# Which queue carries the turned output columns: two layers of a graph network on one core

## The chip, the core and the metric

The kernel runs on one core of a Trainium2 chip. A core has five engines that matter here, each with an instruction stream of its own that it works through in order: TensorE (PE, matmuls), VectorE (DVE), ScalarE (ACT), GpSimd (POOL) and SyncE (SP), which only issues transfers. Transfers (DMA) between the chip's main memory and the core's on-chip memory are carried by 16 DMA engines. A transfer is issued by an instruction in the stream of SP or of ACT, so it takes a place in that engine's order and can wait there. Transfers issued by SP are on queue q1 of the profile, those of ACT on q10. An engine waits for others through semaphores.

The metric is the device time of one execution in microseconds (us); the median of several runs counts.

## The reference

The input is x, 3327 rows of 512 numbers, and adj, a 3327 x 3327 matrix. Everything is in 32-bit floats. Two layers follow each other:

```python
# layer 0
h = relu(layernorm(x))
q, k, v = h @ Wq.T + bq, h @ Wk.T + bk, h @ Wv.T + bv
a = q @ k.T / sqrt(512) + adj + adj
x = x + softmax(a) @ v                      # called x1 below
# layer 1
h = relu(layernorm(x))
A2 = adj + I;  d = diagonal(A2) ** -0.5
temp = A2 @ h @ W.T
x = x + relu((d[:, None] * A2 * d[None, :]) @ temp)
```

So there are three large products with a 3327 x 3327 matrix: the softmax's with v (the kernel applies Wv after it), A2 with h, and A2 with temp. The change concerns the end of the last one, where x1 is added and the output is written.

## The kernel before, in words

The 3327 rows are padded to 26 tiles of 128. They are divided into two strips (of 14 and 12 tiles), and each strip into two halves (`HT` = 7 and 6 tiles, so 896 and 768 columns). `ROW` maps the kernel's tile order to rows.

**The three products.** Each large product (`g` = 0, 1, 2) is computed by a scheme with seven block products instead of eight, applied twice, one inside the other. The outer seven are named in `ORDER` (p5, p1, p6, p7, p2, p3, p4). For each of them and each strip `s` the kernel makes seven steps: `t` = 0 to 5, which take a pair of tiles each, and `t` = None for the thirteenth tile. That is 3 x 7 x 2 x 7 = 294 steps, numbered k = 0 to 293 by `number_of(g, r, s, t)`. A step with a pair issues the seven inner products at line 918, one with the thirteenth tile four products at line 909. Each product shows as two matmul records per weight tile, so x14 or x8 per step. A step's operand tiles (`a`) are read from main memory by `left`: line 829, 832 or 836, two transfers of 384 or 448 KB a step on SP. They land in a ring of five slots. VectorE makes sums of them (`four_sums`, lines 163 to 165) in a ring of three slots. The other factor (`Right.load` and `Right.rows`, lines 856 and 870; `Right.make`) is loaded on SP during the second strip of the product before and the first steps of the first strip, and reused in the second strip.

**Gathering.** At the end of a strip (steps t = 5 and t = None) the banks of the accumulator are combined into the result `cts` by VectorE, beginning with a copy by ScalarE (line 961, `Gather.first`; then lines 962 to 965, `Gather.rest` at 981). Some banks are seeded ahead of the next products from `cts` by ScalarE (line 955, `Gather.seed`). The last bank, p8, is seeded only after that copy, as it takes the bank of p1; the product for p8 is the last of the thirteenth tile's four.

**The output columns.** `cts` holds the result turned: features in the partitions, rows of x along the free dimension. During the last two and a half outer products of g = 2 (from step 252 on) most parts of it are final, and class `Columns` writes them out one at a time: 14 parts (s, y, d), one every three steps, the last one two steps behind its predecessor. One part has four methods, entered in the table `between` with the step at which each is due:

- `load` (two steps ahead): the part of x1 is loaded from main memory into one of two slots (`xp_slots`), in the blocked order in which a turn by 32 x 32 blocks leaves the data. Four transfers of 112 or 96 KB, in pieces of 32 numbers, 128 bytes.
- `turn` (the step itself): VectorE transposes the part in 32 x 32 blocks into a slot of `turn_ring`.
- `scale` (one step later): VectorE applies relu and the scale d.
- `add` (two steps later): VectorE adds x1, and four stores to the output, again in pieces of 128 bytes, are handed to `post`.

The six row tiles from 20 on, of which one half of the features is final only at the very end, go another way: `last_load` (line 1104, the x1 rows on ACT), `turn_last` (transposes on TensorE, line 1110) and `finish` (line 1123 on ACT, line 1124 on VectorE, line 1125 a store on SP or ACT in turn).

**The order of work.** `run(k)` writes step k out for all engines. In it come first the operand loads of step k + 3, then all methods of `between` whose name contains "load", then the step's products, then `deliver(k)`, then the gathering and seeding, then the sums of step k + 2 and the other methods of `between`. Everything is inside `in_order`, which holds each engine, SP and ACT among them, to exactly the order in which its instructions were written.

`post` does not issue a transfer but puts it in the list `posted` with the number of the current step. `deliver(before)` takes entries from the head of the list while their number is below `before`. A store posted in step k is so issued in `deliver(k + 1)`, behind the products of step k + 1, on ScalarE (line 795). In ScalarE's order this is ahead of the copy and the seed of step k + 1, if it has any. At the end, `finish` is called for the six tiles and `deliver(len(steps) + 1)` takes what is left.

The slots: `turn_ring` has the slots mid 10 and mid 11, the first two of `spare`. The slot half 11 holds the bias of v in g = 0 and weights of layer 1 in g = 1 (`other_weights`), and nothing afterwards.

Of the kernel before, what the change touches and what calls it, by code (L numbers as in the profile page):

```python
# [47 lines left out]
def graph_layers_kernel(  # L48
# [30 lines left out]
    nc = tc.nc  # L79
# [21 lines left out]
    def ring(*slots):  # L101

        turn = itertools.cycle(slots)

        def take(shape, name):
            kind, k = next(turn)
            return kind(k, shape, name)

        return take
# [213 lines left out]
    class Turned:  # L323
# [23 lines left out]
        def load(self):  # L347
            k, w = self.k, self.w
            self.other = half(2, [P, 2, BW], "a21")[:, :, :w]
            a11, a12, a22 = hp[k][:, 0], hp[k][:, 1], hp[k][:, 2]  # L350
            for y, blocks in enumerate(((a11, a12), (self.other, a22))):
                c0 = ROW[y * HALF + PACKS[k][0]] * P
                xs = xT[:, c0 : c0 + w].rearrange("(z c p) e -> z p c e", z=2, p=P)
                for z, to in enumerate(blocks):
                    after(nc.sync.dma_start(to, xs[z]), self.row)
            self.norms = []
            for m in range(2):
                self.norms.append(half(m, [P, 2, BW], "norms")[:, :, :w])
                self.loaded = nc.sync.dma_start(
                    self.norms[m], normd[k][m][0:1, : 2 * w].rearrange("a (y e) -> a y e", y=2).to_broadcast([P, 2, w]))  # L360
# [415 lines left out]
    def view(k, j):  # L776
        if k not in parts:
            n = PACKS[k][1]
            parts[k] = large(k, [P, n, 4, Q[0]], f"part{k}")
        return parts[k][:, j]  # L780
# [10 lines left out]
    now = [0]  # L791
    posted = []

    def post(dst, src):
        posted.append((now[0], lambda: nc.scalar.dma_start(dst, src)))  # L795
# [13 lines left out]
    spare = [(mid, k) for k in range(10, 15)]  # L809
# [4 lines left out]
    ts_slots = [lambda k=k: view(2, 1).rearrange("p a w -> p (a w)")[:, k * D : (k + 1) * D] for k in range(3)]  # L814
    ts_slots = itertools.cycle([*ts_slots, *(lambda k=k: mid(k, [P, D], "ts") for k in range(12, 15))])
    xp_slots = itertools.cycle([lambda k=k: view(2, 1)[:, 2 * k : 2 * k + 2].rearrange("p a w -> p (a w)") for k in range(2)])
    turn_ring = ring(*spare[:2])
    xr_last = ring(*((half, k) for k in (4, 5, 6)))
    out_last = ring((half, 12), (half, 13), *spare[2:], (half, 14))

# [306 lines left out]
    class Columns:  # L1127
# [10 lines left out]
        def load(self):  # L1138
            self.x = next(xp_slots)()[:, : H[self.s]]
            for to, rows in self.parts(self.x, x1d[self.s][self.y]):  # L1140
                nc.scalar.dma_start(to, rows)

        def turn(self):
            self.o = turn_ring([P, H[0]], "turned")[:, : H[self.s]]
# [8 lines left out]
        def add(self):  # L1153
            nc.vector.tensor_add(self.o, self.o, self.x)
            r0 = (STRIPS[self.s] + self.y * HT[self.s]) * P
            for of, rows in self.parts(self.o, out[r0 : r0 + H[self.s]]):
                post(rows, of)

    every = (*range(PAIRS), None)
    rights = {(g, r, t): Right(g, r, t) for g in range(3) for r in ORDER for t in every}  # L1160
# [555 lines left out]
```

## Time and profile before

| | us |
|---|---|
| median of 3 runs | 2185.3 (2182.72 to 2186.67) |
| the profiled execution's own time | 2186.69 |
| its span in the profile | 2184.8 |
| busy in the span: TensorE matmuls | 2145.7 (98%) |
| VectorE | 1653.1 (76%) |
| ScalarE | 273.0 (12%) |
| GpSimd | 69.1 (3%) |

Transfers: q1 (issued by SP) 276472 packets with 515.02 MB, q10 (issued by ACT) 123936 packets with 69.62 MB. The loads of x1 columns are 56 transfers on q10 between 1922.0 and 2152.0 us, with a median issue time of 538 ns and a median of 5.1 us to land; the stores of columns are 56 transfers on q10 between 1972.3 and 2174.3 us, with a median issue time of 556 ns and a median of 4.5 us to land.

How to read the profile: times are us from the start of the span, unless ns is written. "L918" is line 918 of the kernel. A line of the timeline gives start, duration, engine, line, operation, output<-input with their shape, how many instructions are merged, and in brackets how long the engine was idle before and what ended that. PE is the matmul part of TensorE, PEld its weight load, which overlaps; ACTq and SPq are the instruction queues of ScalarE and SyncE, where transfers are issued. A releaser is inferred from semaphore events, and a wait for several is put down to the one that came last. The tile called `part` in the profile is one region of on-chip memory that serves the operand ring, the sums, the slots of x1 and parts of `cts`; `p` are accumulator banks. "Clock" is the share of the full TensorE clock that was granted, and the DMA share is the mean busy share of the 16 DMA engines; as packets overlap, it can pass 1.

### The profile page before, as it was taken

How to read it: one execution, taken by the hardware profiler on the slowest of the kernel's cores; microseconds unless marked ns; L12 is line 12 of the kernel's file. 1: busy time of each engine (PE TensorE's matmuls, PEld its weight loads, DVE VectorE, ACT ScalarE, POOL GpSimd, SP SyncE). 2: the span in 40 equal slices, each digit the busy share in tenths (PEclk: the TensorE clock that was granted, in tenths of full speed). 3: DMA queues.
4: the chain of work that ended last, by engine and by line, in shares of the span. 5: the costliest groups of instructions: out<-in, count | busy, mean ns of one | idle time of the engine just before them, and what ended most of it. 6: DMA issues, size and time to landing. Idle time of an engine off the chain costs nothing.

```text
span 2184.8 us, 20926 instructions
## 1 busy us (share of the span) xinstructions
PE 2145.7 (98%) x6272; PEld 1183.8 (54%) x6272; DVE 1653.1 (76%) x3235; ACT 273.0 (12%) x441; POOL 69.1 (3%) x63
## 2 busy tenths in 40 slices
PE   9999999999999999999999999999999999999978
PEld 5555555555555555555455555555666655554534
DVE  7479888889977788877777788785656577776876
ACT  6312111212100000001101000001111100000000
POOL 3000000000004000000111000000000000000000
PEclk9999999999999999999999999999999999999989
DMA  8678988889999999889787899886546468789886
GB/s 301 207 254 300 313 298 287 302 294 314 327 261 329 323 357 322 274 292 315 265 315 256 284 328 355 312 280 204 187 142 205 141 205 291 244 224 234 212 225 153
DMA packets 400530, 586.07 MB, mean 268 GB/s; under 512 B 139788, under 2 KB 273304, under 8 KB 400408
## 3 DMA queue, kind: packets, MB, share of 16 engines
q1 hardware_dynamic: 276472, 515.02, 70.7%
q10 hardware_dynamic: 123936, 69.62, 10.9%
q8 instruction: 52, 0.85, 0.2%
q14 instruction: 70, 0.57, 0.1%
HBM read 416.68 MB, written 167.84 MB: 268 GB/s over the span
## 4 chain that ended last, share of the span: by engine, by line
PE 90%; DMA 4%; DVE 3%; ACTq 1%; issue 1%; ACT 0%; SPq 0%; POOL 0%; DVEq 0%
PE p L918 52%; PE Y L541 13%; PE Z L541 7%; PE p L909 4%; PE p L1025 4%; PE pw L1086 3%; PE X L541 3%; PE Y L397 2%; PE Z L397 1%; DMA part<-sum 1%; DMA part<-x1d 1%; DMA part<-in_adjT_dram 1%; ACTq L795 1%; DMA rows<-row 0%; PE X L397 0%
## 5 line engine op out<-in xcount | busy, mean ns | idle before, releaser
L918 PE MATMUL p<-part,b 128*128 128x448 f32 (+1 forms) x3528 | 1263.7, 514 | 7.5 <-ACT p L955 7.0
L918 PEld LDWEIGHTS p<-part,b 128*128 128x128 f32 x3528 | 672.1, 191 | 553.8 <-issue 296.8
L541 PE MATMUL Y<-qt,hp 128*128 128x448 f32 (+1 forms) x832 | 307.9, 513 | 1.9 <-DVE g L553 1.9
L163 DVE TENSOR_TENSOR part<-part 128x896 f32<-128x896 f32 (+1 forms) x252 | 256.8, 1019 | 67.4 <-DMA part<-sum 22.8
L541 PEld LDWEIGHTS Y<-qt,hp 128*128 128x128 f32 x832 | 158.0, 190 | 134.7 <-issue 72.7
L541 PE MATMUL Z<-qt,hp 128*128 128x384 f32 (+1 forms) x416 | 162.2, 512 | 0.0
L165 DVE TENSOR_TENSOR part<-part,part 128x448 f32<-128x448 f32 (+1 forms) x219 | 129.5, 591 | 14.9
L909 PE MATMUL p<-part,b 128*128 128x448 f32 (+1 forms) x336 | 126.2, 518 | 14.4 <-ACT p L955 14.4
L164 DVE TENSOR_TENSOR part<-part,part 128x448 f32<-128x448 f32 (+1 forms) x219 | 129.4, 591 | 7.2
L541 PEld LDWEIGHTS Z<-qt,hp 128*128 128x128 f32 x416 | 79.0, 190 | 66.2 <-issue 37.9
L545 DVE SCALAR_TENSOR_TENSOR g<-g,Y 128x384 f32<-128x384 f32 (+1 forms) x156 | 91.5, 587 | 29.8 <-PE Y L541 26.5
L909 PEld LDWEIGHTS p<-part,b 128*128 128x128 f32 x336 | 64.1, 191 | 69.2 <-issue 31.7
L961 ACT COPY part<-p 128x384 f32<-128x384 f32 (+1 forms) x33 | 16.6, 502 | 678.9 <-PE p L918 384.1
L962 DVE TENSOR_TENSOR part<-p,part 128x384 f32<-128x384 f32 (+1 forms) x33 | 19.3, 586 | 98.4 <-PE p L918 63.4
L548 ACT ACTIVATE g<-g 128x768 f32<-128x768 f32 (+1 forms) x48 | 43.0, 896 | 345.4 <-DVE g L545 301.5
L541 PE MATMUL X<-qt,hp 128*128 128x384 f32 (+1 forms) x208 | 81.1, 512 | 0.0
L1025 PE MATMUL p<-w,ct 128*128 128x512 f32 x136 | 61.6, 592 | 0.0
L541 PEld LDWEIGHTS X<-qt,hp 128*128 128x128 f32 x208 | 39.5, 190 | 33.1 <-issue 19.3
L190 POOL TENSOR_TENSOR rstd<-ve,mhalf 128x1 f32<-128x1 f32 x46 | 39.3, 857 | 529.9 <-DVE ve L188 502.8
L981 DVE TENSOR_TENSOR ct<-p,part 128x448 f32<-128x448 f32 (+1 forms) x72 | 42.4, 610 | 17.5 <-PE p L909 13.2
L1086 PE MATMUL pw<-w,rows 128*128 128x256 f32 x208 | 53.5, 380 | 0.4 <-DVE rows L1076 0.4
L1016 DVE TENSOR_TENSOR job<-job 128x896 f32<-128x896 f32 (+1 forms) x52 | 53.0, 1019 | 0.0
(194 smaller groups left out, 1682.5 us busy)
## 6 DMA issues: line engine op xcount, KB each, us to landing
part<-sum SPq DMA_DIRECT2D x104, 448.0 KB, 5.3
part<-p SPq DMA_DIRECT2D x91, 448.0 KB, 5.7
part<-sum SPq DMA_DIRECT2D x104, 384.0 KB, 3.8
part<-p SPq DMA_DIRECT2D x91, 384.0 KB, 4.7
part<-in_adjT_dram SPq DMA_DIRECT2D x78, 448.0 KB, 5.2
b<-row SPq DMA_DIRECT2D x234, 128.0 KB, 4.9
part<-in_adjT_dram SPq DMA_DIRECT2D x78, 384.0 KB, 3.6
g<-in_adjT_dram SPq DMA_DIRECT2D x52, 448.0 KB, 4.3
```

Of the source, the lines that this page charges most:

```text
L163: yield nc.vector.tensor_add(o[:, 0:2], g[:, 0:4:3], g[:, 1:2].to_broadcast([P, 2, g.shape[-1]]))
L164: yield nc.vector.tensor_add(o[:, 2], o[:, 1], g[:, 0])
L165: yield nc.vector.tensor_add(o[:, 3], o[:, 2], g[:, 2])
L397: nc.tensor.matmul(ps[:, :w], M[B[name]][:, c, o * P : (o + 1) * P], hp[k][:, A[name], c], start=start and c == 0, stop=c == 1, skip_group ...
L541: nc.tensor.matmul(ps[:, :wd], h_of(self.t, name, k), qt[B[name]][:, k], start=start and k == 0, stop=k == 1, skip_group_check=True)
L545: nc.vector.scalar_tensor_tensor(a[n], a[n], 2.0, ps[:, :wd], op0=ALU.mult, op1=ALU.add if sign > 0 else ALU.subtract)
L548: nc.scalar.activation(g[1], g[1], AF.Exp, **({"bias": pad} if self.t == HALF - 1 else {}))
L909: yield nc.tensor.matmul(ps[("p2", "p3", "p4", "p8")[k]][:, :w], b[:, z], a[:, 0, y], start=k == 3 and not self.seeded, stop=True, skip_gr ...
L918: yield nc.tensor.matmul(ps[r][:, :w], b[:, i], m, start=self.t == 0 and not adds, stop=self.t == PAIRS - 1 and r in ("p1", "p5", "p6", "p ...
L1016: nc.vector.tensor_add(self.a, self.a, self.b)
L1025: nc.tensor.matmul(ps, cts[s][y][d][:, k * P : (k + 1) * P], w[d], start=d == 0, stop=d == DC - 1)
L1086: nc.tensor.matmul(ps, a, W[B[name]][:, c], start=new and c == 0, stop=c == 1, skip_group_check=True)
```

## The change

Three edits:

- `turn_ring` gets a third slot, half 11.
- `Columns.load` issues its four loads of x1 on SP instead of ACT. Their place in the written order stays: step k - 2, behind the operand loads of that step and the loads for the right factor.
- `Columns.add` no longer calls `post`, but puts its four stores into `posted` itself, with the number of the current step plus 2, and to be issued on SP. `deliver` takes them three steps after the add instead of one; those of the last column are taken by the call behind the last step. As the list is taken from its head, what is posted behind such an entry waits for it.

```diff
-    turn_ring = ring(*spare[:2])
+    turn_ring = ring(*spare[:2], (half, 11))
@@ class Columns, load
             for to, rows in self.parts(self.x, x1d[self.s][self.y]):
-                nc.scalar.dma_start(to, rows)
+                nc.sync.dma_start(to, rows)
@@ class Columns, add
             for of, rows in self.parts(self.o, out[r0 : r0 + H[self.s]]):
-                post(rows, of)
+                posted.append((now[0] + 2, lambda rows=rows, of=of: nc.sync.dma_start(rows, of)))
```

## The prediction

> **What bounds the kernel now.** I read the busy shares first, then the chain that ended last, then the last third engine by engine.
>
> ```profile
> PE 2145.7 (98%) x6272; PEld 1183.8 (54%) x6272; DVE 1653.1 (76%) x3235; ACT 273.0 (12%) x441; POOL 69.1 (3%) x63
> ```
>
> TensorE works for 98% of the span, so only what keeps it idle or slow can pay. The chain has the matmuls of lines 909 and 918 in a fixed rhythm (start, duration, what):
>
> ```profile
> 1887.52 31.57 PE p L918 x84
> ...
> 1951.77 31.57 PE p L918 x84
> ...
> 2024.32 33.14 PE p L918 x84
> ...
> 2140.48 3.01 PE p L909 x8
> ```
>
> Undisturbed, one product of two strips lasts 1951.77 - 1887.52 = 64.25 us, and its first strip 31.57 + 3.01. From 1951.77 the first strip of the last product should end at 1951.77 + 2 x 64.25 + 34.58 = 2114.85; it ends at 2143.49. **28.6 us are lost**, all where turned columns are loaded and stored. The timeline of PE names the engine:
>
> ```profile
> 2022.67 1.65 PE L909 MATMUL p<-part,b 128*128 128x384 f32 x2 [7.01 <-ACT p L955]
> ...
> 2097.35 1.65 PE L909 MATMUL p<-part,b 128*128 128x384 f32 x2 [7.40 <-ACT p L955]
> ...
> 2109.19 31.28 PE L918 MATMUL p<-part,b 128*128 128x448 f32 x78 [6.18 <-ACT p L955]
> ```
>
> With a wait of 0.20 at 2062.59 that is 20.8 us of waiting; the other 7.8 are slow matmuls behind each wait (two take 1.65 us, where six of the same form took 2.10 before it; x84 take 33.14 instead of 31.57). What ScalarE did meanwhile is in its timeline, where ACTq is its queue of instructions:
>
> ```profile
> 1997.65 5.98 ACTq L795 DMA_DIRECT2D out_dram<-turned  x4
> 2004.84 9.54 ACTq L1141 DMA_DIRECT2D part<-x1d  x4
> 2016.30 5.28 ACTq L795 DMA_DIRECT2D out_dram<-turned  x4
> 2021.62 0.48 ACT L961 COPY part<-p 128x384 f32<-128x384 f32 x1 [32.54 <-DMA out_dram<-turned]
> 2022.13 0.49 ACT L955 ACTIVATE p<-ct 128x384 f32<-128x384 f32 x1
> ```
>
> TensorE finished the step at 2013.57; the copy and the seed for the last bank, half a microsecond each, stood behind eight DMA issues until 2021.62. The four stores were ready from 2003.6 (their add starts at 2002.65): they stood behind the loads, and the loads behind landings, since the chain runs from one landing to the next issue (store issued 1999.18, 5.63 us; loads 2004.84, 7.01 us, and 2011.87, 5.84 us). The transfers are crowded there (length, PE, PEld, DVE, ACT and POOL busy, clock, DMA share, GB/s):
>
> ```profile
> 1750.00:1920.00 170.00, 170.00 (x483) 91.61 (x483) 124.27 (x239) 7.16 (x14) 0.00 (x0) 1.00 0.72 239
> 1983.00:2025.00 42.00, 34.96 (x103) 19.66 (x102) 24.52 (x40) 2.29 (x5) 0.00 (x0) 0.95 1.06 242
> ```
>
> [...] between 1983 and 2016 the column loads take a median 6.8 to 7.0 us to land, over the whole run at best 2.5. [...] I count no byte as saved. [...] columns go in pieces of 128 B. Between 1983 and 2016 q10 moved 1.73 MB with 37.0% of the engines' time and q1 6.77 MB with 72.6%: 4.7 against 9.3 MB per full share, half the rate. [...]
>
> **The change part by part.**
>
> *Loads and stores leave ACT.* 14 columns x 4 = 56 loads and 56 stores. ACT then holds only copies, seeds and, at the end, xr loads and three output stores. The three waits on ACT go, and with them the slow matmuls: -28.6 us. The seed then follows a step's end by copy and seed, 0.49 + 0.49 us, and is needed only after six matmuls of the thirteenth tile, 2.10 us: hidden.
>
> *They join SP.* Median issue 0.54 (load) and 0.56 us (store): 112 x 0.55 = 62 us on SP. Between 1920 and 2180 SP waits 71.8 + 38.0 + 6.8 + 6.1 + 3.0 = 125.7 us for TensorE to free operand slots; that hides the 62 on average. Not everywhere: in 1983 to 2016 these waits are only 12.2 us for some 16 issues (9 us), so the cover is nearly used up. What stands behind them on SP are operand loads (L832, L836) and right factors (L856, L870), for which DVE's sums and then TensorE wait. Their reserve: a load issued at 1998.93 lands for the sum at 2005.93, DVE ends its sums at 2008.4, and TensorE would need them, undelayed, at 2013.57 + 3.01 = 2016.6: **8.2 us**. A column issued at its best, 4 x 0.55 = 2.2 us, is hidden in it; uncovered it would cost 2.2 for each half column.
>
> *DMA time.* Unchanged in bytes, but now in a shorter time. The highest share that holds for some time is 1.12 (1996 to 2016). The stretch 1983 to 2025 carries 1.06 x 42 = 44.5, or 39.7 us at 1.12; TensorE's own work in it is 34.96: 4.8 us too much. 2057 to 2110 carries 0.87 x 23 + 0.93 x 30 = 47.9, or 42.8 us; TensorE's 22.8 + 16.4 less some 3.8 for the slow clock is 35.4: 7.4 too much. Both lie under the reserve of 8.2, so the least is 0; with no reserve it is 12.2 us and about 5 for a slow clock again. I take **+4**, as the second comes close and carries over from the first.
>
> *Stores two steps later.* A store queued in step j is issued in step j+3 of SP's order, whose operand load waits for TensorE to be done with step j+1. DVE's add of step j is over by then, as DVE has to make the sums of step j+2 ahead of it; only after a gather (a step with t = 5) it may be 1 us late. Issued in j+1, the store would hold SP for most of a step (4.5 us): that is the cost if this cover were gone. At nothing.
>
> *Third slot (half 11).* A column is turned every 3 steps; its store is issued 5 steps after its turn and takes a median 3.6 to 5.0 us. Two slots come round after 6 steps, about when it lands; three after 9, some 3 steps (13.5 us) in hand. The slot's earlier tile belongs to the weights of the stage before. Nothing.
>
> *x slots.* Two remain: a load waits for the add of the column before last. Normally that is two steps old; only for the last column one step, where SP may wait up to 4 us, with two operand steps left to load. Nothing.
>
> *Tail.* Now the last four column stores start at 2172.73 on ACT, and the first of six output activations waits for them:
>
> ```profile
> 2172.73 2.42 ACTq L795 DMA_DIRECT2D out_dram<-turned  x4
> 2176.00 1.57 ACT L1123 ACTIVATE r<-pt,sd 128x256 f32<-128x256 f32 x4 [8.78 <-DMA out_dram<-turned]
> ```
>
> Its transposes run from 2173.22 to 2175.38, so ACT can start near 2173.7 and end with them, about 2.4 us earlier; SP's three output stores come behind four column stores (2.2 us), which takes some back: -1.8. Bounds -2.5 and +2.
>
> Sum against the profiled execution, 2186.69 us (span 2184.8): 2186.69 - 28.6 + 4 - 1.8 = 2160.3. That execution is 1.4 above the median of 2185.3; the forecast is **2160**.
>
> **The rivals.**
> - *Transfers take the waits' place* (part of the gain): [...] the reserve doesn't carry. For: shares of 1.06 and over, SP's waits of 12.2 us. Against: DVE's 8.2 us. With the 12.2 + 5 above it gives 2186.7 - 28.6 + 17 - 1.8 = 2173.
> - *SP blocks as ACT did* (slower): the four loads hold SP as long as they held ACT at worst (9.54) and the stores 5.98, 15.5 us a column, beside a dozen other issues of 0.42 (5 us): 20.5 in three steps of 4.52 (13.6), 7 late; with six issues 18 in 15.8, 2 late. Some 7 columns of each kind: 49 + 14 = 63, less 2 x 8.2 reserve, gives 2186.7 - 30.4 + 47 = 2203. It decides once a column holds SP longer than 13.6 - 5 = 8.6 us (15.8 - 2.5 = 13.3 in the loose strips). Against: the pair's medians make 4.4; the long ones on ACT were waits for landings.
> - *No change*: ACT was only the messenger, and the crowded transfers hold seed and operands all the same, so as many microseconds come back on DVE's sums. For: the chain before the first wait is made of landings. Against: the copy was ready to run at 2013.57 whatever landed. 2185.
>
> **How the numbers follow.** Forecast case 0.62 (2152 to 2167: from no late transfer at all, 2156, less the spread of the three runs, to 10 us late); partial 0.21 (2167 to 2181); no change 0.04; slower 0.13. The range 2152 to 2180 leaves out the last two and the edge of the second. A change of 0.2%, 4.4 us, is what this kernel's measurement can tell from none. Faster 0.83, same 0.04, slower 0.13.
>
> **What would show it.** Right: no wait of PE on ACT p L955 above 1 us from 1950 on, PE's rhythm near 64.25 throughout, the last turned stores on SP and the first output activation right behind its transposes. The +4 is right if DVE's L163 or b waits a few us on DMA near the last product's start. Wrong: SP's queue with column issues of 2 us and more each, DVE's sums waiting on part<-in_adjT_dram or b<-row in every third step, and PE waiting for DVE; or new SP waits on DVE's add L1154, which would mean that two steps are too few.

## The result and the profile after

The changed kernel takes 2169.03 us (median of 4 runs, 2168.21 to 2169.72) beside 2184.2 us of the kernel before in the same session: a ratio of 0.9929 with a 95% interval of 0.9912 to 0.9946, so 15 us or 0.7% faster. The profiled execution took 2169.72 us, its span is 2167.9.

The page's first part, and from the chain that ended last the starts of the last five outer products (start, duration, what):

```profile
PE 2142.5 (99%) x6272; PEld 1182.1 (55%) x6272; DVE 1653.3 (76%) x3235; ACT 273.1 (13%) x441; POOL 68.4 (3%) x63
```

```profile
1824.88 31.57 PE p L918 x84
...
1889.13 31.57 PE p L918 x84
...
1953.38 31.57 PE p L918 x84
...
2017.62 31.57 PE p L918 x84
...
2081.87 20.31 PE p L918 x54
```

From 1824.88 to 2081.87 the distance is four times 64.25 us to the hundredth: up to the start of the last product nothing is lost any more. Before, two products in this stretch came 8.3 and 10.4 us late. The timeline of PE shows what is left, all in the last product:

```profile
2109.69 4.78 PE L918 MATMUL p<-part,b 128*128 128x448 f32 x12 [0.76 <-DVE part L164]
2114.31 3.17 PE L909 MATMUL p<-part,b 128*128 128x448 f32 x8
2121.46 30.08 PE L918 MATMUL p<-part,b 128*128 128x384 f32 x84 [3.98 <-DVE part L962]
2151.38 2.74 PE L909 MATMUL p<-part,b 128*128 128x384 f32 x8
```

No wait on ACT p L955 stands there. The two that do are waits for VectorE, and the 84 matmuls behind the second take 30.08 us where they took 27.25 in undisturbed strips.

One measure serves for all runs below. From a product's undisturbed start (1824.88 here) five products of 64.25 us lead to the last matmul of line 909, 321.25 us later. What a run needs beyond that is its **loss**; from there to the end of the span is its **tail**. After: 2151.38 + 2.74 - 1824.88 - 321.25 = 8.0 us lost, and a tail of 2167.9 - 2154.12 = 13.8. Before, from 1823.27: 28.6 lost, and a tail of 11.7. The start itself lies between 1820.5 and 1825.4 in the profiles below, though the kernels do the same work up to there; why single executions differ by that much was not looked into. So a difference in time between two runs is only partly loss and tail.

### The profile page after: what moved, and what is told of

The parts are those of the page before. It is cut to its first block, busy times and chain, and to the rows that moved or that the text cites. A ratio compares the mean times of both kernels' runs of the same rounds, so it can differ in the third digit from the quotient of the medians.

```text
span 2167.9 us, 20907 instructions
## 1 busy us (share of the span) xinstructions
PE 2142.5 (99%) x6272; PEld 1182.1 (55%) x6272; DVE 1653.3 (76%) x3235; ACT 273.1 (13%) x441; POOL 68.4 (3%) x63
## 2 busy tenths in 40 slices
DMA packets 400530, 586.07 MB, mean 270 GB/s; under 512 B 139788, under 2 KB 273304, under 8 KB 400408
## 4 chain that ended last, share of the span: by engine, by line
PE 90%; DVE 5%; DMA 3%; issue 1%; SPq 0%; POOL 0%; ACT 0%; DVEq 0%
PE p L918 52%; PE Y L541 13%; PE Z L541 6%; PE p L909 5%; PE p L1025 4%; PE pw L1086 3%; PE X L541 3%; PE Y L397 2%; PE Z L397 1%; DMA part<-in_adjT_dram 1%; DVE part L163 1%; DMA part<-p 1%; DMA rows<-row 0%; PE X L397 0%; DMA wk<-in_wk_dram 0%
## 5 line engine op out<-in xcount | busy, mean ns | idle before, releaser
L165 DVE TENSOR_TENSOR part<-part,part 128x448 f32<-128x448 f32 (+1 forms) x219 | 129.5, 591 | 14.9
L981 DVE TENSOR_TENSOR ct<-p,part 128x448 f32<-128x448 f32 (+1 forms) x72 | 42.5, 609 | 18.2 <-PE p L909 13.8
```

The costliest lines, as they stand in the source:

```text
L165: yield nc.vector.tensor_add(o[:, 3], o[:, 2], g[:, 2])
```

## The experiments

All kernels of a group ran on one chip with the kernel before beside them. The ratio is to that; loss and tail come from one profile each.

| run | median us | ratio (95% interval) | loss | tail |
|---|---|---|---|---|
| before | 2184 to 2186 | 1 | 28.6 | 11.7 |
| after | 2169.0 | 0.9929 (0.9912 to 0.9946) | 8.0 | 13.8 |
| only the stores moved | 2166.1 | 0.9909 (0.9893 to 0.9926) | 8.4 | 12.9 |
| only the loads moved | 2176.5 | 0.9963 (0.9948 to 0.9977) | 14.9 | 15.1 |
| later stores and third slot, all on ACT | 2181.8 | 0.9974 (0.9964 to 0.9985) | 21.7 | 12.0 |
| after, stores not later | 2181.4 | 0.9977 (0.9966 to 0.9988) | 19.9 | 11.9 |
| after, two slots | 2165.3 | 0.9906 (0.9888 to 0.9923) | 7.8 | 11.3 |
| after, xr loads on SP too | 2164.7 | 0.9900 (0.9883 to 0.9916) | 4.3 | 13.8 |
| before, a quarter of each column transfer | 2159.8 | 0.9875 (0.9856 to 0.9894) | 2.6 | 10.6 |
| after, a quarter of each column transfer | 2158.1 | 0.9868 (0.9852 to 0.9885) | 0.0 | 10.2 |
| after, long pieces | 2162.5 | 0.9887 (0.9870 to 0.9903) | 6.3 | 9.5 |
| xr on SP, last stores not later | 2164.3 | 0.9903 (0.9886 to 0.9919) | 3.8 | 14.2 |
| xr on SP, column loads on GpSimd | 2161.9 | 0.9885 (0.9869 to 0.9902) | 3.9 | 13.5 |
| the last two together | 2161.3 | 0.9880 (0.9863 to 0.9896) | 3.8 | 11.2 |

After reading the changed kernel's trace I had a theory for the remaining loss and a rival. It rests on a listing of the transfers that SP issues near 2104 us in the compiled program (number, line, transfer, semaphores waited for):

```
1560 L1141 DMACopy part2_3621<-x1d10_147 32x24x32 [waits DMAHW1_49,DVE_49]
1561 L1141 DMACopy part2_3621<-x1d10_147 32x24x32 [waits DMAHW3_49]
1562 L1141 DMACopy part2_3621<-x1d10_147 32x24x32 [waits DMAHW1_49]
1563 L1141 DMACopy part2_3621<-x1d10_147 32x24x32 [waits DMAHW2_49]
1564 L836 DMACopy part0_3572<-in_adjT_dram 128x768 [waits DMAHW3_49,PE_49]
```

DMAHW0 to DMAHW7 are eight completion semaphores that this program deals in turn to the transfers of *both* queues. The trace has them as numbers 100, 102 and 104 to 109: all of SP's 1608 transfers and ACT's 194 carry one of these eight, each number occurs on both engines, and 1671 of the 1802 wait, before their issue, on the number that they carry themselves. The five above carry 102, 105, 102, 104 and 105. The numbers skipped (DMAHW2, and 4 to 0; in the trace 104, 106 to 109 and 100) went to the six xr loads, which are still on ACT. So instruction 1562 waits for the landing of 1560: the last update of 102 comes at 2110.22 us and the issue at 2110.24. And 1563 waits for an xr load on another engine: 104 at 2111.81, the issue at 2111.82. The kernel before deals the same eight numbers to SP's 1496 transfers and ACT's 306, and that is how ScalarE came to wait for landings there: its load at 2011.87 waits on 109, which the load issued at 2004.84 updates for the last time at 2011.85. In the trace this is what happened; SP's timeline first, then ACT's, then SP's waits from 2103 to 2113 us (sum, times, longest):

```profile
2103.95 8.18 SPq L1141 DMA_DIRECT2D part<-x1d  x4
2112.23 0.94 SPq L836 DMA_DIRECT2D part<-in_adjT_dram  x2
```

```profile
2108.97 0.53 ACT L961 COPY part<-p 128x448 f32<-128x448 f32 x1 [25.09 <-PE p L918]
2109.53 0.55 ACT L955 ACTIVATE p<-ct 128x448 f32<-128x448 f32 x1
2109.67 2.79 ACTq L1104 DMA_DIRECT2D xr<-x1d  x6
```

```profile
SPq L1141 <- DMA part<-x1d: 5.3, 1, 5.3
SPq L1141 <- DMA xr<-x1d: 1.3, 1, 1.3
```

The xr loads stand behind the step's copy and seed, which wait for TensorE. SP's four column loads took 8.18 us. Of these, 5.3 went by until load 1560 landed, whose semaphore came round so soon because the xr loads had used six; only 1.3 went by waiting for an xr load itself. The operand load behind them went out from 2112.23 on and took 5.7 us to land; VectorE sat idle for it, and that is the 3.98 us of TensorE:

```profile
2118.66 0.96 DVE L163 TENSOR_TENSOR part<-part 128x768 f32<-128x768 f32 x1 [6.09 <-DMA part<-in_adjT_dram]
```

The *ring theory* says that the rest of the loss is this holding of one queue by the other. The *traffic theory* says that SP and the DMA engines are full with small pieces, so that operands are late in any case. The trace has both at once: the wait of 5.3 us comes from the dealing and from a slow landing.

**Which half of the move counts.** The first two runs do one half each.

```diff
# only the stores moved: after, with
-                nc.sync.dma_start(to, rows)
+                nc.scalar.dma_start(to, rows)
```

> Stores on SP, two steps later, with the third slot; the loads of x1 stay on ACT. Ring theory (ScalarE's copy and seed are late because an issue ahead of them waits for the landing of an earlier transfer of either queue): the loads alone still hold ACT, but end earlier, since no store stands between them and the copy; one or two waits of PE on the seed of 1 to 4 us remain, 2174 us. Traffic theory [...]: SP has half of the added issues, so operands are on time and the last product has no wait of PE on DVE, 2165 us.

```diff
# only the loads moved: before, with
-                nc.scalar.dma_start(to, rows)
+                nc.sync.dma_start(to, rows)
```

> Loads of x1 on SP, stores as before on ACT one step after the add, two slots. Ring theory: the stores are ready when ACT comes to them, but wait for landings and hold the copy by one group (5 us) where the add comes just before it; one or two waits of PE on the seed, 2174 us, and the tail of before (first output activation behind the last store). Traffic theory: 2165 us, no wait of PE on DVE in the last product.

Stores alone on SP are as good as both: 2166.1 us, loss 8.4. The time is next to the traffic theory's 2165, though its "no wait on VectorE" fails: there is one of 2.4 us. The waits on the seed that the ring theory wanted are there too, but small (two on ACT p L955, 3.4 us in all), and its 2174 is missed. Loads alone leave more than half as much to lose as before (14.9 of 28.6): the ring theory's 2174 is nearer to 2176.5 than the rival's 2165, and the waits on the seed are 1.17 and 4.45 us. So either half takes issues away from in front of the copy. The stores look like the better half, but the first run also has the later stores and the third slot, and the second has neither; the next run shows that these two alone are worth 4 to 6 us, which is part of the 10 us between the halves.

**The later stores.** First alone on ACT, then the changed kernel without them.

```diff
# later stores and third slot on ACT: before, with
-    turn_ring = ring(*spare[:2])
+    turn_ring = ring(*spare[:2], (half, 11))
-                post(rows, of)
+                posted.append((now[0] + 2, lambda rows=rows, of=of: nc.scalar.dma_start(rows, of)))
```

> The kernel before with only the later stores and the third slot; loads and stores stay on ACT. If ACT's lateness came from waiting for the add of a column: gone, below 2170 us. Traffic theory (it comes from landings that are slow because the small pieces fill the engines, and as many issues stand before the copy): PE's waits on the seed stay above 10 us in all, 2180 to 2186 us.

```diff
# stores not later: after, with
-                posted.append((now[0] + 2, lambda rows=rows, of=of: nc.sync.dma_start(rows, of)))
+                posted.append((now[0], lambda rows=rows, of=of: nc.sync.dma_start(rows, of)))
```

> The changed kernel with the stores posted with the current step's number, so issued on SP one step after the add instead of three. SP runs ahead of VectorE, so each group of stores makes it wait for the add, at most most of a step (4.5 us), 14 times; with operands late in the crowded stretches: ring theory 2190 us, with SP waiting on L1154 for 30 us and more in all. Traffic theory: the same transfers in nearly the same time, 2170 us.

On ACT the delay and the third slot bring 4 us by the medians and 6 by the ratio, and TensorE still waits 7.21, 9.17 and 0.51 us for the seed, 16.9 of 20.8: ACT's lateness was for the most part not the wait for an add. On SP the delay is worth 10 us by the ratios and 12 by the medians; the runs without it lie far apart (2174.9 to 2188.9). SP's list of waits without it:

```profile
SPq L1157 <- DVE turned L1154: 31.4, 7, 11.3
```

That is the 30 us expected, 24.0 of it up to 2140 us; the changed kernel has 6.2 us of it in two waits, both at the very end, when no operand load is left. The loss grows by 11.9 us (19.9 against 8.0), so a good part of the waits falls into slack. The delay isn't all that differs in the profile: SP also waits 8.2 us for xr loads before column loads, where it waits 1.3 in the changed kernel.

**The third slot.**

```diff
-    turn_ring = ring(*spare[:2], (half, 11))
+    turn_ring = ring(*spare[:2])
```

> The changed kernel with two slots for turned tiles again. A slot then comes round after six steps and its store is issued five steps after the turn, so the turn of column n waits for the landing of the stores of column n-2: VectorE waits for it up to a landing (5 us) where SP is late, and its sums with it. Traffic theory: SP is late in the last two products, so this bites, 2180 us. If the slots were never short: 2169 us.

The loss is the same, 7.8 against 8.0. VectorE waits for a landing of stores twice, for 1.26 and 0.97 us, inside its slack. The profiled execution is shorter by an earlier start (1821.43) and a shorter tail, and the intervals of the two ratios overlap: the third slot gains nothing that these runs show.

**What holds the last product.** The xr loads go to SP; then the pieces are made fewer, or longer. Where a transfer brings only a quarter, the slots are cleared once at the start.

```diff
# xr loads on SP too: after, with
-            nc.scalar.dma_start(xr[:, k], x1_of(i + k)[:, 0:E])
+            nc.sync.dma_start(xr[:, k], x1_of(i + k)[:, 0:E])
```

> The changed kernel, with the six xr loads (line 1104) on SP too, so that ScalarE issues no transfer before the last outputs. Ring theory (SP stood from 2104.9 to 2112.2 because its transfers waited for semaphores that the xr loads held, and these waited in ACT for a step's end): the waits of PE on DVE of 0.76 and 3.98 us and the slow matmuls behind them go, 2169.0 - 7.5 = 2161.5 us. Traffic theory (SP and the DMA engines are full there in any case): 2167 to 2170 us, the waits of PE stay.

The 3.98 us wait becomes three of 0.2 to 0.5, and the loss falls from 8.0 to 4.3; by time alone the gain is not clear, as the intervals of the two ratios touch. It is half of what the ring theory promised. TensorE still waits 0.67 us for a seed and 1.20 for VectorE, and VectorE is idle for an operand load for 2.34 us at 2116.20 instead of 6.09. SP's timeline has the column loads and the first xr loads:

```profile
2104.63 6.11 SPq L1141 DMA_DIRECT2D part<-x1d  x4
2135.77 0.90 SPq L1104 DMA_DIRECT2D xr<-x1d  x2
```

The four column loads still hold SP for 6.11 us, where they held it for 8.18, and SP's list of waits has none over 2.2 us for an xr load. And the edit does more than free the semaphores. ACT had run ahead and issued the xr loads at 2109.67; in SP's order they come 26 us later, so their 0.79 MB are also gone from the stretch where the late operand load lands. These runs don't tell the two apart.

```diff
# a quarter of each column transfer, on before and on after
+    primed = []
...
-        return [(tile[32 * a : 32 * a + 32].rearrange("r (j e) -> r j e", e=32), rows[self.d, a]) for a in range(4)]
+        q = HT[self.s]
+        return [(tile[32 * a : 32 * a + 32].rearrange("r (j e) -> r j e", e=32)[:, 0:q], rows[self.d, a, :, 0:q]) for a in range(4)]
...
             self.x = next(xp_slots)()[:, : H[self.s]]
+            if len(primed) < 2:
+                primed.append(nc.gpsimd.memset(self.x, 0.0))
```

> The changed kernel with every column transfer cut to a quarter: as many transfers, each with a quarter of its 128-byte pieces (three quarters of x1 aren't added and three quarters of these output columns aren't stored). Traffic theory (the rest of the loss in the changed kernel is the small packets' time on the DMA engines): the last product's waits go and the time is 2157. Ring theory alone (the rest is SP standing behind the xr loads of ScalarE): SP still stands until the step's end near 2109, a wait of PE of some 2 us and slow matmuls remain, 2161 to 2163.

> The kernel before with every column transfer cut to a quarter, as in the run above (three quarters of x1 aren't added and three quarters of these columns aren't stored); the order and the number of transfers on ACT and SP stay. If ACT is late because the landings it waits for are slowed by traffic: the waits of PE on the seed shrink from 20.8 us to under 5, 2160. If ACT is late because of the order and the number of its issues: over 10 us of these waits remain, 2175 or more.

With as many transfers in the same written order, and a quarter of the pieces and so of their bytes, the changed kernel has no loss at all, and the kernel *before* loses 2.6 us instead of 28.6, with one wait left of its 20.8 us:

```profile
2086.99 29.58 PE L918 MATMUL p<-part,b 128*128 128x448 f32 x78 [2.38 <-ACT p L955]
```

So the landings that ACT waited for were slow because of the column transfers' own traffic: the stores land after a median of 2.9 us instead of 4.5, the longest issue of a store on ACT falls from 3.76 to 0.60 us, and the median only from 0.56 to 0.45. The place of the issues decided who paid for it.

In the changed kernel with a quarter of the pieces SP still stood for the xr loads, as the ring theory said, but before operand loads (its timeline):

```profile
2105.65 8.01 SPq L836 DMA_DIRECT2D part<-in_adjT_dram  x4
```

No wait of TensorE came of it. The operand load that is late in the changed kernel had gone out before, at 2101.52, and VectorE did not wait for the next. SP's two waits before operand loads for xr loads make 7.9 us here, where the changed kernel has 1.3 us before a column load: the holding falls on other transfers, so this run doesn't show what it costs where it falls in the changed kernel.

```diff
# long pieces: after, with
-            rows = rows.rearrange("(j r) (c a e) -> c a r j e", r=32, a=4, e=32)
-            return [(tile[32 * a : 32 * a + 32].rearrange("r (j e) -> r j e", e=32), rows[self.d, a]) for a in range(4)]
+            w = H[self.s]
+            rows = rows.rearrange("n f -> (n f)").rearrange("(c a r w) -> c a r w", c=4, a=4, w=w)
+            return [(tile[32 * a : 32 * a + 32], rows[self.d, a]) for a in range(4)]
```

> The changed kernel, its column transfers with the same bytes, but each partition's row in one contiguous piece of 3584 or 3072 bytes instead of 28 or 24 pieces of 128 (the values then come from and go to other places of x1 and the output). If the pieces' number is what the engines pay for: no wait of PE in the last product, 2158 us as with a quarter of the pieces. If it is the bytes, or SP's issues and waits: 2165 to 2169 us.

The time, 2162.5, fell between the two answers, but the profile separates them. The same stretch of two kernels, by windows (length, the busy times of PE, PEld, DVE, ACT and POOL, clock, DMA share, GB/s), after and then with long pieces:

```profile
2018.00:2050.00 32.00, 32.00 (x86) 16.18 (x86) 26.45 (x47) 1.28 (x3) 0.00 (x0) 1.00 1.10 251
```

```profile
2018.00:2050.00 32.00, 32.00 (x86) 16.15 (x85) 26.52 (x46) 1.54 (x3) 0.00 (x0) 1.00 0.81 252
```

The same bytes at the same rate take a share of 0.81 instead of 1.10: it is not the bytes but the form of the pieces that fills the engines. (Their addresses lie together now, too; the runs don't separate this from their number.) With that gone, one wait of 4.54 us remains on TensorE, and SP shows whose it is:

```profile
SPq L1142 <- DMA xr<-x1d: 11.3, 1, 11.3
```

SP is early now, and stands 11.3 us for an xr load on ACT. Neither theory alone explains the last product's 8 us: moving the xr loads leaves 4.3, lengthening the pieces leaves 6.3. The two gains of 3.7 and 1.7 don't add up to 8, and no run does both at once, so there is no clean split. Most of what long pieces gain in the profiled execution is in the tail (13.8 to 9.5), not in the loss (8.0 to 6.3).

**The tail and a better kernel.**

```diff
# last stores not later: xr loads on SP, and
-                posted.append((now[0] + 2, lambda rows=rows, of=of: nc.sync.dma_start(rows, of)))
+                posted.append((now[0] + 2 * (now[0] < number_of(2, 6, 0, 6)), lambda rows=rows, of=of: nc.sync.dma_start(rows, of)))
# column loads on GpSimd: xr loads on SP, and
-                nc.sync.dma_start(to, rows)
+                nc.gpsimd.dma_start(to, rows)
```

> All x1 loads and the xr loads on SP, and the stores of the last three columns posted without the two steps of delay, as no operand load stands behind them any more. If the tail (11 us from the last transpose to the end, 9.4 before the change) is long because SP still issues column stores ahead of the last outputs: 2 us less than with the xr loads on SP alone, 2162.7. If the tail is bound by the last column's own four stores: no difference, 2164.7.

> As the run with the xr loads on SP, but the column loads of x1 are issued by GpSimd, which is idle then, so they are in no line with SP's or ACT's transfers. If what is left is SP's place in line (issues and waits for landings): the last product has no wait of PE, 2158. If it is the engines' traffic: as with SP, 2164. [...]

> Column loads on GpSimd, xr loads on SP, stores on SP with no delay for the last three columns. If the two gains add: 2160 us. If the shorter delay again makes SP wait for VectorE while its last operand loads are due: 2162 us or more.

Shorter delays at the end bring nothing that can be told (2164.3 against 2164.7). Its profile shows a gain and a loss: 8.4 us from the last transpose to the end instead of 11.3, but the transposes begin 2.67 us late, behind VectorE. GpSimd as the issuer gives 2161.9, between the expected 2158 and 2164, and not clear of the run with only the xr loads moved (their intervals overlap): each of its issues takes a steady 0.72 to 0.92 us, the loads land after a median 6.9 us, and VectorE's list of waits from 1920 on has none for them. Both together give 2161.3; the ratio of 0.9880 (0.9863 to 0.9896) lies clear of the changed kernel's interval (0.9912 to 0.9946), so this kernel beats the changed one as well as the one before. One wait on the seed (1.90 us) and the slow matmuls behind it are its whole loss; they follow a wait of VectorE for the last product's first operands.

## Why the prediction was right, and where it was off

The measured 2169.0 lies in the range (2152 to 2180) and on the forecast side. It lies above the likeliest case's own range (2152 to 2167), inside that of the rival "transfers take the waits' place", of which a part came true; it is the wide range that holds it, not the likeliest case. Against the working, with the profiled execution: 2160.3 + 4.0 (loss) + 3.9 (tail) + 1.6 (a later start at 1824.88 instead of 1823.27) = 2169.8; it took 2169.72.

- *-28.6 for loads and stores leaving ACT*: right to the hundredth up to the last product. The step named waits for landings as ACT's trouble, and a quarter of the pieces frees the kernel before of 26 of its 28.6 us. That the move saves no byte was right too (586.07 MB in both), but bytes are not all here: who waits in which line was worth 15 us.
- *+4 for transfers that come late*: mis-sized, 8.0. It comes at the end of the second crowded stretch (2109 to 2121 us), not near the last product's start. With the xr loads out of the way 4.3 are left, but that this is the forecast number is partly luck: 4 was a choice between 0 and 17, not a sum. The rest has a cause that the step left out: the xr loads stayed on ACT, and with the semaphores shared, SP stood 6.6 us (5.3 for its own load's landing, 1.3 for an xr load). I had read such couplings in the trace of before, a load waiting for a store's landing, and priced them only for the transfers that move.
- *62 us of issues under 125.7 us of SP's waits*: mis-sized. 112 times a median leaves out the long issues and the waits between them: the groups of column loads and stores in SP's timeline add up to 136 us, more than the 125.7 (on ACT before, where it could have been read, 138). SP's waits for TensorE shrank to 36.2 us between 1920 and 2165, with about 5 us of it from 2018 to 2109. A column's four loads held SP 2.03 to 8.18 us and its four stores 3.67 to 5.44; together 9 to 11 us in most columns of the crowded strips (5.16 + 3.92, 6.19 + 3.86), past the slower rival's deciding point of 8.6. The time did not turn all the same: up to 2109 none of SP's lateness ended in a wait of TensorE, where the rival let it add up from column to column.
- *Stores two steps later at nothing*: right, and the cover was needed: without it 10 to 12 us come back.
- *Third slot at nothing*: right. *Two x slots at nothing, up to 4 us for the last column*: SP did wait for adds before loads, 6.3 us in two waits, but of 4.3 and 2.0 us and long before the last column; no wait of TensorE follows them.
- *Tail -1.8*: wrong in sign, +2.1 (13.8 against 11.7). The first output activation does run right behind its transposes (2155.54, with transposes from 2154.71), as forecast. What failed is "SP's three output stores come behind four column stores (2.2 us)": the term counts issues and leaves out a wait for a landing. SP's timeline, then its wait (sum, times, longest):

```profile
2138.70 17.93 SPq L1157 DMA_DIRECT2D out_dram<-turned  x12
2160.54 2.77 SPq L1125 DMA_DIRECT2D out_dram<-r  x3
```

```profile
SPq L1125 <- DMA out_dram<-r: 3.8, 1, 3.8
```

The delay piles up twelve column stores, but SP is through with them at 2156.63, before VectorE has made the last outputs (2158.30). Then it waits 3.8 us for the landing of an output store that ACT issued, whose semaphore its own store takes next (number 109 in the trace: its last update comes at 2160.48 us, SP's store goes out at 2160.54). Its output stores so begin 6.4 us after the last matmul of line 909, where they began 3.8 after it before the change. With long pieces, behind the same twelve stores, this wait is absent and the tail is 9.5; no run takes the wait away alone.

- *No change* is refuted: with the issues moved, the crowded transfers cost 8 us, not 28.6.

## What to carry to other kernels

When an engine that computes also issues transfers, look at what it issues ahead of the short instruction that everybody waits for (20.8 us of TensorE's waits here). A queue that only issues can stand in line as long as there is slack behind it: up to 2109 us none of SP's lateness ended in a wait of TensorE. A store is best issued when its data is sure to be there, which was worth 10 to 12 us. Before counting issues on the new queue, count the transfers that stay on the old one: with eight semaphores dealt over both, SP stood 6.6 us here (5.3 for its own load's landing, 1.3 for an xr load), and moving the six loads left behind took the loss from 8.0 to 4.3 us. To reckon what issues cost a queue, add up the groups in its timeline (136 us here), not a median times their number (62). And when a stretch is crowded, ask for the form of the pieces before the number of bytes: the same bytes in long pieces brought about as much as the best reordering (2162.5 and 2161.3 us).

## What the runs showed that was not expected

- Pieces of 128 bytes cost the DMA engines a share of 0.29 more (1.10 against 0.81) at the same 251 to 252 GB/s, with only some transfers in such pieces.
- Only the stores on SP, with the loads on ACT, are as good as all on SP (loss 8.4 and 8.0). Two queues with four issues each a column served no worse here than one with eight.
- Behind a wait of 3.98 us of TensorE the next 84 matmuls took 2.8 us longer (30.08 against 27.25), with a granted clock of 0.50 from 2121.5 to 2126. Shorter waits are not alike: 1.90 us in the last kernel was followed by 31.28 us for 78 matmuls, 2.38 us in the kernel before with a quarter of the pieces by 29.58, with a granted clock of 1.00 from 2082 to 2109. Why slower matmuls followed the shorter wait and not the longer stays open.
- GpSimd issued transfers of 768 to 896 pieces in 0.72 to 0.92 us each without a long one, while SP took 0.30 to 3.60.
